# First layer's dispatch loads input rows and normalises them on ACT; first input in four pieces; output weights scaled inside the loop

## The chip, the cores and the metric

The kernel is one program on one core of a Trainium2 chip. The metric is device time in microseconds (us) of the whole program, the median of several runs. All tensors are float32. TensorE is called PE here, VectorE DVE, ScalarE ACT, GpSimd POOL, and SP is the engine that issues most of the DMA transfers.

## What is computed

Two layers, each of the same outer form, on 4096 rows of 256 numbers:

```python
xn = layernorm(x)
x = x + L0_attn(xn, ...) + L0_ffn(xn, ...)     # layer 0
xn = layernorm(x)
x = x + L1_attn(xn, ...) + L1_ffn(xn, ...)     # layer 1
```

`L0_attn` is a state-space mixer: one projection gives a gate (2048 channels), h (2048), B and C (128 each) and a step size dt for each of 32 heads; h, B and C pass a causal convolution of four taps and a silu; dt passes softplus; then a scan over the rows, in which each head's state decays by exp(A dt). The output is multiplied by silu(gate), divided by its root mean square, multiplied by `norm_w` for each channel, and projected by `W_out` to 256.

`L0_ffn` is a mixture of 16 experts. A row goes to the best four experts of its two best groups, and two shared experts take every row:

```python
g = silu(einsum('th,efh->tef', x, w1_e)); u = einsum('th,efh->tef', x, w3_e)
routed = einsum('tef,ehf,te->th', g * u, w2_e, combine)
```

Here x is the normalised row xn. Layer 1 has a linear attention with batch norms and a mixture of 8 experts, two for each row; the change touches it only by a name.

## The kernel before

**The start (0 to about 100 us).** Rows are taken in eight groups of 512, as 128 partitions x 4 tiles x 256. For each group `fetch` (L868) loads the input (`xin`), and `norm_block` (L156) runs in three parts with a `yield` between. First come the mean and variance of each tile on DVE (`st`, `mv`, L162 to L164), a square root on ACT (`rs`, L165), a reciprocal on DVE (L166) and the normalised rows `xn` on DVE (L168). Then `xn` is written to DRAM (`xn_d`, L172) and transposed on PE (`pt`, L176), and ACT copies the result to `xt` (L179), which also goes to DRAM (`xT_d`). Last comes a small projection on PE (`pr`) to 32 step sizes and 16 router scores, which DVE takes out (`take0`). For each quarter of the rows `sizes` (L886) turns the step sizes into decays: `e_t` and `a_row` by exp, `l_t` by ln, `u_t` by exp (L901), then `adt`, `rows` and `dec`. Square root, exp, ln and silu need different tables on ACT. Between these, SP loads the weights (`weights()`), of which `w_o` is the output projection, and `rows_sb`, a small row of constants.

In the start the program's order on SP and DVE is the order of the code (a manual schedule); on ACT, PE and POOL a scheduler sets the order. Before the loop begins, the first projections `pj`, convolutions (`cv` on ACT L371 and DVE L373, then silu to `hc` and `bc`), and `hdt` and `hd` of the first half step are made. At L999 to L1002 POOL multiplies the sixteen slices of `w_o` by `norm_w` (`n_ch`).

**The loop (L1045).** It has 128 half steps: 16 blocks of 256 rows, by four groups of eight heads, by two halves of 128 rows. In each, PE makes projections (`pj` L363, `pg` L433), the state's update (`pst`, in `advance`), the mixer's output (`py` L561) and the output projection (`po` L595); DVE does the taps and a scan (`mm` L468); POOL multiplies `mm` by the B-C products (`masked`, L517), `g` by the gate (`gate_y`, L1019) and `hdt` by its decay (`hd`, L507); SP fetches the decays of later halves (`mm<-step_d`, `cs<-from_d`). Six calls of `point()` in a half step are places where other work is mixed in, and that work has three stages:

- In the first half steps the router's choice runs, with 0 to 2 pieces per point, and large fills of the expert buffers with zeros (one issue per half step).
- From half step 14 (`FILLED`) on, `dispatch0` (L676) advances twice in a half step, at its fourth and sixth point. For each of 32 tiles of 128 rows it loads the normalised rows from `xn_d` into `xs` one tile ahead, POOL copies the row's tail of routing data behind them, and four indirect DMAs, issued by POOL, write the rows to the places of their four experts. One tile takes two half steps.
- When `dispatch0` has ended, the 82 steps of the expert pipeline (79 blocks of 256 rows and 3 to drain it; `blocks`, four generators) are spread over the half steps that are left: `t = ceil(todo / remaining)`, so two per half step at first and one at the end.

```python
elif sends is not None and k >= FILLED:
    points[3], points[5] = sends, sends
elif ticks is not None and todo:
    t = min(todo, -(-todo // max(len(half) - 1 - k, 1)))
```

In the first two stages the code's order holds on POOL and SP, in the third on all engines. An engine takes its instructions in order, so one that waits holds up all behind it. In one half step POOL's order around the change is: `masked` (two `mm`), then `gate_y` of the half step before, then `hd` of the next.

**Behind the loop** the shared experts run (with rows from `xT_d`), then layer 1, whose dispatch loads its rows from `xn_d` at L1255.

Of the kernel before, what the change touches and what calls it, by code (L numbers as in the profile page):

```python
# [10 lines left out]
FP = mybir.dt.float32  # L11
# [90 lines left out]
def two_layer_kernel(  # L102
# [43 lines left out]


    xT_d = [dram.tile([P, KD, FB], FP, name=f"xT_d{g}") for g in range(NFB)]
    xn_d = [[dram.tile([FB, DM], FP, name=f"xn_d{lay}_{g}") for g in range(NFB)] for lay in (0, 1)]

    xg0_d = dram.tile([NB0 * RB, RW0], FP, name="xg0_d")
    xg1_d = dram.tile([NB1 * RB, RW1], FP, name="xg1_d")
# [3 lines left out]
    def norm_block(g, lay, src, work, bank, w_r, n_r, take, xn, xt, copies):  # L156


        mv = work.tile([P, TPB, 2], FP, tag="mv", name=f"mv{g}", bufs=2)
        rs = work.tile([P, TPB], FP, tag="rs", name=f"rs{g}", bufs=2)  # L160
        for j in range(TPB):
            st = work.tile([P, 6], FP, tag="st6", name=f"st{g}_{j}", bufs=4)  # L162
            nc.vector.bn_stats(st, src(j))
            nc.vector.bn_aggr(mv[:, j, :], st)  # L164
        nc.scalar.activation(rs, mv[:, :, 1], AF.Sqrt, bias=eps_t)  # L165
        nc.vector.reciprocal(rs, rs)  # L166
        for j in range(TPB):
            nc.vector.tensor_scalar(  # L168
                xn[:, j, :DM], src(j), mv[:, j, 0:1], rs[:, j : j + 1], ALU.subtract, ALU.mult
            )  # L170
        yield
        nc.sync.dma_start(xn_d[lay][g].rearrange("(j p) d -> p j d", p=P), xn)  # L172
        for k in range(KD):
            pt = bank(f"pt{g}_{k}", False)
            for j in range(TPB):
                nc.tensor.transpose(  # L176
                    pt[:, j * P : (j + 1) * P], xn[:, j, k * P : (k + 1) * P], ident
                )
            copies[k](xt[:, k, :], pt)  # L179
        yield  # L180
        pr = bank(f"pr{g}", True)
        prv = pr.rearrange("p (j n) -> p j n", j=TPB)
        for j in range(TPB):
            for k in range(KD):
                nc.tensor.matmul(
                    prv[:, j, :n_r],
                    xt[:, k, j * P : (j + 1) * P],
                    w_r[:, k, :],
                    start=(k == 0),
                    stop=(k == KD - 1),  # L190
                )
        take(g, prv)
# [109 lines left out]
    from_d = [dram.tile([NTP * HEADS, P], FP, name=f"from_d{p}") for p in range(PARTS)]  # L302
    w_o = wpool.tile([P, NCI, DM], FP, name="w_o")
    sc = wpool.tile([P, NT, E0], FP, name="sc")
    blank = wpool.tile([P, RPB, RW0], FP, name="blank")
    nc.gpsimd.memset(blank, 0.0)
    nc.gpsimd.iota(
# [34 lines left out]
    with tc.tile_pool(name="m", bufs=1) as mp, tc.tile_pool(  # L342
# [169 lines left out]
        def masked(n, j, blk):  # L512

            mm = rows_in[n * CPB + j]
            for q in range(GH // QH):
                m = mm[:, q * QH : (q + 1) * QH, :]
                nc.gpsimd.tensor_tensor(m, m, mid(blk["gm"][j], QH), ALU.mult)  # L517
            return mm
# [157 lines left out]
        def dispatch0():  # L676

            def load(i):
                if i < NT:
                    xs = moe.tile([P, RPB * DM], FP, tag="ys", name=f"xs0_{i}", bufs=3)[:, :RW0]  # L680
                    o = i % TPB * P
                    nc.sync.dma_start(xs[:, :DM], xn_d[0][i // TPB][o : o + P, :])
                    ahead.append(xs)

            ahead = []
            load(0)
            yield
            for i in range(NT):
                load(i + 1)
                xs = ahead.pop(0)  # L690
                nc.gpsimd.tensor_copy(xs[:, DM:], tail0[:, i, :])
                for k in range(TOPK0):
                    nc.gpsimd.indirect_dma_start(
                        out=views0[i * TOPK0 + k],
                        out_offset=bass.IndirectOffsetOnAxis(ap=dest0[:, i, k : k + 1], axis=0),
                        in_=xs,
                        in_offset=None,
                        bounds_check=NB0 * RB - 1,
                    )
                    yield  # L700
# [167 lines left out]
        def fetch(g):  # L868
            if g < NFB:
                t = mp.tile([P, TPB, DM], FP, tag="mm", name=f"xin{g}", bufs=3)  # L870
                nc.sync.dma_start(
                    t, x[g * FB : (g + 1) * FB, :].rearrange("(j p) d -> p j d", p=P)
                )
                xin.append(t)

        def take0(g, prv):
# [119 lines left out]
        ahead()  # L996
        ahead()
        decays(0, 0)
        for c in range(NCI):  # L999
            nc.gpsimd.tensor_scalar(  # L1000
                w_o[:, c, :], w_o[:, c, :], n_ch[:, c : c + 1], 0.0, ALU.mult, ALU.add
            )  # L1002
        for e in early:
            whole(e)
        side.close()
# [10 lines left out]
        def gate_y(k):  # L1016
            if k >= 0:
                n, j = half[k]
                nc.gpsimd.tensor_tensor(  # L1019
                    gs[k], gs[k], gates[n][:, :, j * P : (j + 1) * P], ALU.mult  # L1020
                )
# [23 lines left out]
        for k, (n, j) in enumerate(half):  # L1045
            blk = blks[steps[n][0]]
            next(fill, None)
            points, t = [None] * 6, 0
            if routing is not None:
                for _ in range(3):  # L1050
                    if next(routing, side) is side:
                        side.close()
                        moe = side.enter_context(tc.tile_pool(name="moe", bufs=1))
                        routing, sends = None, dispatch0()
                        break
# [4 lines that stand above are left out]
                if t == 1:  # L1060
                    points[0], points[2], points[4] = ticks[:3]
                else:
                    points = ticks[:3] * t
                todo -= t

            def point():
                nonlocal sends, ticks
                q = points.pop(0)
                if q is not None and next(q, done) is done and q is sends:
                    sends, ticks = None, [blocks(at) for at in range(4)]  # L1070
                    ordered.close()
                    ordered.enter_context(tc.manual_schedule())

            if begun is not None:
                second, begun = begun, None
            else:
                second = None
            conv, gate = (n + 1 + j, 1 - j), (n + j, 1 - j)
            if conv[1] == 0 and conv[0] < len(steps) and steps[conv[0]][1] == 0:
                begun = begin(steps[conv[0]][0])  # L1080
                next(begun)
            late(k - 1)
            ahead()
            old = state[steps[n][1]]
            ahead_of = projections(conv, gate)
            at_once = ticks is not None
            if at_once:
                advance(n, j, blk, made[k][1])
            next(ahead_of, None)
            point()  # L1090
            if not at_once:
                advance(n, j, blk, made[k][1])
            ys[k] = old, masked(n, j, blk)
            gate_y(k - 1)
            if t:
                next(ticks[3])
            if over:
                finish(over.pop())
            next(ahead_of, None)
            point()  # L1100
            next(ahead_of, None)
            if k + 1 < len(half):
                n1, j1 = half[k + 1]
                made[k + 1] = inputs(n1, j1, hcs[n1])
            point()
            next(ahead_of, None)
            if second is not None:
                whole(second)
            next(ahead_of, None)
            if begun is not None:  # L1110
                next(begun)
            point()
            out_ = project(*half[k - 3], gs.pop(k - 3)) if k >= 3 else iter(())
            next(out_, None)
            if begun is not None:
                next(begun)
            point()
            whole(out_)
            if k + 1 < len(half):
                decays(*half[k + 1])  # L1120
            while points:
                point()
            if t > 1:
                next(ticks[3])
# [111 lines left out]
    def route1():  # L1236
# [15 lines left out]
        for g in range(NFB):  # L1252
            tl = slice(g * TPB, (g + 1) * TPB)
            xs = wk.tile([P, TPB, RW1], FP, tag="xs", name=f"xs{g}")
            nc.sync.dma_start(xs[:, :, :DM], xn_d[1][g].rearrange("(j p) d -> p j d", p=P))  # L1255
            nc.gpsimd.memset(xs[:, :, DM:RW], 0.0)
            nc.gpsimd.tensor_copy(xs[:, :, DM], ids_t[:, tl])
            nc.gpsimd.tensor_copy(xs[:, :, RW:], comb1[:, tl, :])
# [341 lines left out]
```

## Time and profile before

| what | value |
|---|---|
| median of three runs | 2353.54 us (2347.74, 2353.54, 2356.76) |
| profiled execution's own time | 2359.07 us |
| its span / granted TensorE clock | 2357.2 us / 0.966 |
| PE busy | 2182.1 us, 93% |
| PE weight load (PEld) busy | 1728.1 us, 73% |
| DVE busy | 1460.2 us, 62% |
| ACT busy | 920.9 us, 39% |
| POOL busy | 1486.4 us, 63% |
| DMA | 412.17 MB, 175 GB/s |

An engine's busy time is the sum of its instructions' durations; its share is an average over stages that differ much. PE's matmul times are modelled, so 93% is not PE at its peak. The span in 40 slices of 59 us shows the stages (each digit is the busy share in tenths):

```profile
PE   6687999999999998999999989999799989999998
DVE  6799988888888887555565656677356542111111
POOL 0345699888888988677777777888541461323222
```

The first two slices are the start and the loop's first half steps. From there to slice 15 or so the rows are routed and sent out; then the expert blocks run beside the mixer until about slice 27; the rest is the shared experts and layer 1. The transfers that the change touches are, in the profile's list of DMA issues (KB each, median us from issue to landing):

```profile
xn_d<-xn SPq DMA_DIRECT2D x16, 512.0 KB, 7.2
xin<-in_x SPq DMA_DIRECT2D x8, 512.0 KB, 5.5
xs<-xn_d SPq DMA_DIRECT2D x32, 128.0 KB, 5.6
```

### The profile page before, as it was taken

How to read it: one execution, taken by the hardware profiler on the slowest of the kernel's cores; microseconds unless marked ns; L12 is line 12 of the kernel's file. 1: busy time of each engine (PE TensorE's matmuls, PEld its weight loads, DVE VectorE, ACT ScalarE, POOL GpSimd, SP SyncE). 2: the span in 40 equal slices, each digit the busy share in tenths (PEclk: the TensorE clock that was granted, in tenths of full speed). 3: DMA queues.
4: the chain of work that ended last, by engine and by line, in shares of the span. 5: the costliest groups of instructions: out<-in, count | busy, mean ns of one | idle time of the engine just before them, and what ended most of it. 6: DMA issues, size and time to landing. Idle time of an engine off the chain costs nothing. (4 is left out here: it accounts for less than half of the span.)

```text
span 2357.2 us, 36770 instructions
## 1 busy us (share of the span) xinstructions
PE 2182.1 (93%) x12684; PEld 1728.1 (73%) x12684; DVE 1460.2 (62%) x3356; ACT 920.9 (39%) x1907; POOL 1486.4 (63%) x1294
## 2 busy tenths in 40 slices
PE   6687999999999998999999989999799989999998
PEld 5565777777777777777777868788566568888887
DVE  6799988888888887555565656677356542111111
ACT  5632443343334333444443434444223752222221
POOL 0345699888888988677777777888541461323222
PEclk8799999999999999999999999999899999999999
DMA  9577679544444445677777777766451347777775
GB/s 307 195 216 213 194 232 259 174 143 153 143 136 155 145 133 169 158 181 165 181 178 168 189 175 176 177 169 164 134 188 54 107 158 215 188 202 189 199 195 116
DMA packets 247435, 412.17 MB, mean 175 GB/s; under 512 B 41552, under 2 KB 184912, under 8 KB 242640
## 3 DMA queue, kind: packets, MB, share of 16 engines
q1 hardware_dynamic: 198240, 347.24, 47.7%
q0 software_dynamic: 42336, 57.04, 13.8%
q10 hardware_dynamic: 6672, 5.51, 0.7%
q8 instruction: 103, 1.69, 0.3%
q14 instruction: 84, 0.69, 0.1%
HBM read 293.19 MB, written 116.52 MB: 174 GB/s over the span
## 5 line engine op out<-in xcount | busy, mean ns | idle before, releaser
L373 DVE SCALAR_TENSOR_TENSOR cv<-pj,cw,cv 128x256 f32<-128x256 f32 x864 | 402.5, 477 | 99.1 <-ACT cv L371 90.0
L517 POOL TENSOR_TENSOR mm<-mm,btok 128x512 f32<-128x512 f32 x256 | 341.6, 1435 | 13.3 <-DVE mm L468 12.5
L468 DVE TENSOR_TENSOR_SCAN mm<-mm,eyes 128x256 f32<-128x256 f32 x512 | 318.0, 667 | 24.3 <-ACT eyes L474 24.3
L363 PE MATMUL pj<-xt,w_in 128*128 128x259 f32 (+1 forms) x1152 | 315.4, 399 | 11.6 <-DVE pj L359 7.3
L433 PE MATMUL pg<-xt,w_in 128*128 128x256 f32 x1024 | 281.7, 397 | 32.3 <-ACT gate L440 29.7
L777 POOL DMA_INDIRECT moe_d<-ys,ids x158 | 248.9, 1575 | 98.4 <-DMA moe_d<-ys,ids 42.3
L1492 POOL DMA_INDIRECT out<-ys,ids x72 | 111.0, 1541 | 301.6 <-ACT ys L1488 267.5
L363 PEld LDWEIGHTS pj<-xt,w_in 128*128 128x128 f32 x1152 | 218.1, 196 | 79.8 <-issue 35.0
L595 PE MATMUL po<-w_o,g 128*128 128x256 f32 x1024 | 261.5, 389 | 0.0
L433 PEld LDWEIGHTS pg<-xt,w_in 128*128 128x128 f32 x1024 | 188.9, 196 | 90.3 <-ACT gate L440 39.2
L1476 DVE TENSOR_TENSOR hid<-silu,pu 128x512 f32<-128x512 f32 x72 | 49.5, 688 | 321.6 <-PE pu L1470 321.6
L371 ACT ACTIVATE cv<-pj,cw 128x256 f32<-128x256 f32 x288 | 135.5, 471 | 240.0 <-PE pj L363 239.4
L507 POOL TENSOR_TENSOR hd<-hdt,dec 128x512 f32<-128x512 f32 x124 | 144.4, 1165 | 121.6 <-DVE hdt L498 117.5
L595 PEld LDWEIGHTS po<-w_o,g 128*128 128x128 f32 x1024 | 193.9, 195 | 28.1 <-issue 2.7
L1019 POOL TENSOR_TENSOR g<-g,gate 128x512 f32<-128x512 f32 x128 | 180.4, 1409 | 50.4 <-DVE g L572 27.6
L384 ACT ACTIVATE hc<-cv,bw 128x256 f32<-128x256 f32 x256 | 129.2, 505 | 160.6 <-DVE cv L373 160.4
L747 PE MATMUL pgu<-xgt,w 128*128 128x256 f32 x632 | 155.6, 390 | 18.6 <-DVE state L543 18.6
L472 DVE TENSOR_TENSOR cs<-cs,eyes 128x512 f32<-128x512 f32 x248 | 159.2, 671 | 0.0
L587 ACT ACTIVATE g<-g 128x512 f32<-128x512 f32 x128 | 80.8, 632 | 200.7 <-POOL g L591 147.6
L572 DVE SCALAR_TENSOR_TENSOR g<-hc,ch,py 128x128 f32<-128x128 f32 x512 | 144.3, 339 | 22.2 <-PE py L561 22.0
L561 PE MATMUL py<-cs,state 128*64 128x128 f32 x1984 | 145.5, 286 | 13.3 <-issue 9.8
L561 PEld LDWEIGHTS py<-cs,state 128*64 128x64 f32 x1984 | 111.3, 141 | 59.8 <-issue 54.3
(245 smaller groups left out, 4063.8 us busy)
## 6 DMA issues: line engine op xcount, KB each, us to landing
mm<-step_d SPq DMA_DIRECT2D x128, 512.0 KB, 5.0
cs<-from_d SPq DMA_DIRECT2D x124, 512.0 KB, 6.1
w<-in_w_ffn SPq DMA_DIRECT2D x36, 1024.0 KB, 5.9
w<-in_w_ffn SPq DMA_DIRECT2D x79, 384.0 KB, 3.3
xg_d<-blank SPq DMA_DIRECT2D x26, 828.0 KB, 9.3
xg<-xg_d SPq DMA_DIRECT2D x79, 260.0 KB, 4.3
w<-in_w_ffn SPq DMA_DIRECT2D x36, 512.0 KB, 6.6
xg_d<-blank SPq DMA_DIRECT2D x18, 536.0 KB, 9.6
```

The costliest lines, as they stand in the source:

```text
L363: nc.tensor.matmul(pj[:, h0 : TB + HALO], w_in[:, k, INTER + c * P : INTER + (c + 1) * P], xts[b][:, k, h0 : TB + HALO], start=(k == 0), s ...
L373: nc.vector.scalar_tensor_tensor(cv, pj[:, i : i + TB], cw[:, c, i : i + 1], cv, ALU.mult, ALU.add)
L433: nc.tensor.matmul(pj[:, :TB], w_in[:, k, c * P : (c + 1) * P], xts[b][:, k, HALO:], start=(k == 0), stop=(k == KD - 1),)
L468: nc.vector.tensor_tensor_scan(m, m, eye, 0.0, ALU.mult, ALU.add)
L472: nc.vector.tensor_tensor(m, m, mid(c_in[:, j, :], QH), ALU.mult)
L507: nc.gpsimd.tensor_tensor(hd, hdt, last(dec[c // NTP][:, 0, c % NTP, hs], HP), ALU.mult)
L517: nc.gpsimd.tensor_tensor(m, m, mid(blk["gm"][j], QH), ALU.mult)
L561: nc.tensor.matmul(py[(h % 2) * HP : (h % 2 + 1) * HP, h // 2, :], left[:, h, :], right[:, h, :], start=(a == 0 and h < 2), stop=(a == len ...
L595: nc.tensor.matmul(po[:, j, :], g[:, i, :], w_o[:, k, :], start=(k == 0 and j == 0), stop=(k == NCI - 1), skip_group_check=True,)
L747: nc.tensor.matmul(pgu[:, a, :], w[:, o : o + P], xgt[:, k, :], start=(k == 0), stop=(k == KD - 1),)
L777: nc.gpsimd.indirect_dma_start(out=moe_d[:, :], out_offset=bass.IndirectOffsetOnAxis(ap=ids[:, j : j + 1], axis=0), in_=ys[:, j, :], in_of ...
L1019: nc.gpsimd.tensor_tensor(gs[k], gs[k], gates[n][:, :, j * P : (j + 1) * P], ALU.mult)
```

## The change

1. `norm_block` writes the normalised rows to DRAM in layer 1 only. In layer 0 two small DVE instructions per group keep `rs` (one over the deviation) and `-mean * rs` of every row in `norm0`.
2. `dispatch0` loads rows of the input x instead of `xn_d`, and ACT normalises them in place (activation Identity with a scale and a bias per row) before they are sent: tile i + 1 after the second send of tile i. The first tile has a step of its own, so the generator has one `yield` more.
3. The first group's input is fetched in four pieces of 128 rows instead of one of 512.
4. The scaling of `w_o` on POOL (16 instructions) moves from ahead of the loop into half step 1, between `masked` and `gate_y`.
5. At L1255 layer 1 reads the renamed `xn_d`.

```diff
@@ norm_block
-        nc.sync.dma_start(xn_d[lay][g].rearrange("(j p) d -> p j d", p=P), xn)
+        if lay:
+            nc.sync.dma_start(xn_d[g].rearrange("(j p) d -> p j d", p=P), xn)
+        else:
+            tl = slice(g * TPB, (g + 1) * TPB)
+            nc.vector.tensor_copy(norm0[:, 0, tl], rs)
+            nc.vector.scalar_tensor_tensor(
+                norm0[:, 1, tl], mv[:, :, 0], -1.0, rs, ALU.mult, ALU.mult
+            )
@@ dispatch0
-                    o = i % TPB * P
-                    nc.sync.dma_start(xs[:, :DM], xn_d[0][i // TPB][o : o + P, :])
+                    nc.sync.dma_start(xs[:, :DM], x[i * P : (i + 1) * P, :])
                     ahead.append(xs)
+
+            def normed(i):
+                if i < NT:
+                    xs = ahead[-1]
+                    nc.scalar.activation(
+                        xs[:, :DM], xs[:, :DM], AF.Identity, bias=norm0[:, 1, i : i + 1],
+                        scale=norm0[:, 0, i : i + 1],
+                    )
 
             ahead = []
             load(0)
+            yield
+            normed(0)
             yield
             for i in range(NT):
                 load(i + 1)
                 xs = ahead.pop(0)
                 nc.gpsimd.tensor_copy(xs[:, DM:], tail0[:, i, :])
                 for k in range(TOPK0):
+                    if k == 2:
+                        normed(i + 1)
                     nc.gpsimd.indirect_dma_start(
@@ fetch
-                nc.sync.dma_start(
-                    t, x[g * FB : (g + 1) * FB, :].rearrange("(j p) d -> p j d", p=P)
-                )
+                v = x[g * FB : (g + 1) * FB, :].rearrange("(j p) d -> p j d", p=P)
+                for j in range(0, TPB, TPB if g else 1):
+                    m = TPB if g else j + 1
+                    nc.sync.dma_start(t[:, j:m, :], v[:, j:m, :])
@@ ahead of the loop
-        for c in range(NCI):
-            nc.gpsimd.tensor_scalar(
-                w_o[:, c, :], w_o[:, c, :], n_ch[:, c : c + 1], 0.0, ALU.mult, ALU.add
-            )
@@ in the loop's half step
             ys[k] = old, masked(n, j, blk)
+            if k == 1:
+
+                for c in range(NCI):
+                    nc.gpsimd.tensor_scalar(
+                        w_o[:, c, :], w_o[:, c, :], n_ch[:, c : c + 1], 0.0, ALU.mult, ALU.add
+                    )
             gate_y(k - 1)
```

More of the change, by code (lines that the diff above doesn't have):

```diff
@@ L148, in two_layer_kernel @@
     xT_d = [dram.tile([P, KD, FB], FP, name=f"xT_d{g}") for g in range(NFB)]
-    xn_d = [[dram.tile([FB, DM], FP, name=f"xn_d{lay}_{g}") for g in range(NFB)] for lay in (0, 1)]
+    xn_d = [dram.tile([FB, DM], FP, name=f"xn_d{g}") for g in range(NFB)]
     xg0_d = dram.tile([NB0 * RB, RW0], FP, name="xg0_d")
@@ L304, in two_layer_kernel @@
     sc = wpool.tile([P, NT, E0], FP, name="sc")
+    norm0 = wpool.tile([P, 2, NT], FP, name="norm0")
     blank = wpool.tile([P, RPB, RW0], FP, name="blank")
@@ L1254, in route1 @@
             xs = wk.tile([P, TPB, RW1], FP, tag="xs", name=f"xs{g}")
-            nc.sync.dma_start(xs[:, :, :DM], xn_d[1][g].rearrange("(j p) d -> p j d", p=P))
+            nc.sync.dma_start(xs[:, :, :DM], xn_d[g].rearrange("(j p) d -> p j d", p=P))
             nc.gpsimd.memset(xs[:, :, DM:RW], 0.0)
```

## The prediction

> **What bounds the kernel now.** I read first the busy time by stretch of the start (columns: stretch, its length, busy us and instructions of five engines, granted clock, share of the DMA engines, GB/s).
>
> ```profile
> 20.00:40.00 20.00, 13.80 (x62) 11.58 (x61) 13.97 (x52) 13.92 (x21) 0.10 (x1) 1.00 1.01 361
> 40.00:60.00 20.00, 13.88 (x69) 11.66 (x68) 11.22 (x42) 12.28 (x20) 0.18 (x2) 0.63 0.94 309
> 80.00:100.00 20.00, 11.38 (x42) 8.32 (x42) 16.86 (x40) 18.47 (x31) 0.10 (x1) 0.83 0.39 118
> 120.00:140.00 20.00, 16.04 (x86) 11.89 (x85) 19.14 (x44) 5.51 (x11) 6.62 (x6) 0.91 0.51 147
> ```
>
> Until 80 us the transfers are full and no engine is, so the start looks bound by transfers. The waits of 0 to 105 us (us in total, times, longest) deny it:
>
> ```profile
> PE pt L176 <- DVE xn L168: 13.5, 4, 9.4
> DVE e_t L903 <- ACT u_t L901: 9.7, 4, 4.7
> DVE rs L166 <- ACT rs L165: 9.4, 8, 2.4
> DVE st L163 <- DMA xin<-in_x: 4.7, 1, 4.7
> ACT xt L179 <- DMA xT_d<-xt: 1.3, 2, 0.8
> ```
>
> TensorE waits for VectorE, VectorE for ScalarE, ScalarE for its tables. A transfer holds an engine of this chain only at the very start (4.7) and for 1.3 us in all. The start is a chain of small steps, and the order on ACT decides. Third, ACT's instructions in order of time (start, us):
>
> ```profile
> 22.36 0.30 ACT L165 ACTIVATE rs<-mv,eps_t 128x4 f32<-128x4 f32 x1 [4.13 <-DVE mv L164]
> 22.91 1.07 ACT L179 COPY xt<-pt 128x512 f32<-128x512 f32 x2 [0.25 <-PE pt L176]
> 24.00 1.28 ACT L894 ACT_TABLE_LOAD   x1
> 25.30 0.42 ACT L894 ACTIVATE e_t<-e_t 128x256 f32<-128x256 f32 x1
> 25.73 1.28 ACT L165 ACT_TABLE_LOAD   x1
> 27.12 0.30 ACT L165 ACTIVATE rs<-mv,eps_t 128x4 f32<-128x4 f32 x1
> 27.96 1.07 ACT L179 COPY xt<-pt 128x512 f32<-128x512 f32 x2 [0.55 <-DMA xT_d<-xt]
> ```
>
> rs of block 3 goes ahead of the copies of xt 2, and rs of block 4 (27.12) ahead of both copies of xt 3. Fourth, POOL at the loop's first halves, and the later stages by hundred us:
>
> ```profile
> 111.23 2.48 POOL L517 TENSOR_TENSOR mm<-mm,btok 128x512 f32<-128x512 f32 x2
> 114.19 1.59 POOL L1019 TENSOR_TENSOR g<-g,gate 128x512 f32<-128x512 f32 x1 [0.48 <-DVE g L572]
> 116.54 1.42 POOL L507 TENSOR_TENSOR hd<-hdt,dec 128x512 f32<-128x512 f32 x1 [0.76 <-DVE hdt L498]
> 130.14 1.27 POOL L1019 TENSOR_TENSOR g<-g,gate 128x512 f32<-128x512 f32 x1 [9.30 <-DVE pj L359]
> ```
>
> ```profile
> 600.00:700.00 100.00, 95.40 (x641) 75.16 (x642) 84.31 (x186) 37.10 (x82) 87.05 (x83) 0.95 0.42 139
> 1300.00:1400.00 100.00, 94.50 (x580) 76.33 (x579) 59.63 (x127) 43.31 (x110) 78.14 (x60) 0.98 0.74 182
> 1500.00:1600.00 100.00, 98.24 (x658) 81.64 (x659) 75.45 (x160) 46.09 (x108) 83.75 (x67) 1.00 0.67 165
> ```
>
> TensorE, VectorE and POOL are all near full while rows are sent out (600); with expert blocks, two per half step (1300) wait more than one per half step (1500).
>
> **The change part by part.** Instruction orders are those of the built programs, durations those of the profiled run.
>
> *No normalised rows written.* Eight transfers of 512 KB go, 4.19 MB, at the 306 GB/s mean of 0 to 80 us 13.7 us of transfer. But engines waited 1.3 us for transfers, of which 0.55 lies ahead of l_t on the chain; in the new order both copies come behind other waits. Value 0, between -1.3 and 0. The rival below says what if transfers decide.
>
> *16 small VectorE operations for norm0.* Nearest rows: 128x3 copies 0.15, reciprocal 0.18; at most 16 x 0.18 = 2.9. They stand before VectorE's waits for TensorE or ACT (2.48 at 30.0, 2.58 at 40.2, 3.65 at 58.6), which cover them. Value 0, up to 2.
>
> *First input in four pieces.* Four issues instead of one put rows_sb's issue at 0.83 + 4 x 0.47 + 0.50 = 3.2 instead of 1.87. ACT's first instruction waits for rows_sb (until 5.82) and the first rs is queued behind it, so VectorE's earlier statistics (to 1.6 earlier) gain little. The same bytes lie ahead of rows_sb: I let it land at 6.1; then eyes, table 6.7 to 8.0, rs 8.0 instead of 8.31: -0.3. A rule speaks against it: the Trainium skill, "DMA: Bandwidth & Descriptors", section "Bandwidth", asks for batches of 1 MiB and lists 64 KB at 138 GB/s; estimated from that, four pieces one after another take 3.8 us where the row's 512 KB landed 3.8 after issue[...], and rs would be about 1.3 later. The row is nearer (issue 0.47, landing 3.8). Range -1.4 to +1.3.
>
> *A new order on ACT in the start.* The schedule now has rs 3 behind the copies of xt 2, and the first copy of xt 3 ahead of e_t, whose table load and rs 4 stand behind it. On PE, pr 2 now runs whole ahead of pt 3; before, they were mixed, 23.55 to 28.59, so pt 3 ends there. Then: copy 28.4 to 29.0, table to 30.3, e_t to 30.7, second copy to 31.3, table to 32.6, rs 4 at 32.6 instead of 27.12: +5.5. After it xn 4 ends at 34.5 and u_t at 37.5 instead of 32.50, since one of two tables is now loaded while ACT would wait: +5.0. From there the order is as before up to block 7, so it stays. Bounds +3 to +6.
>
> *Two more table loads.* 88 instead of 86. At 67 us cv 16 moves ahead of u_t: it waits for pj until 67.64, so u_t ends at 69.8 instead of 67.13 and adt at 72.7 instead of 69.23; then bc 16 and 17 are split around rows, with 1.28 twice more: dec ends at 76.0 instead of 72.72, e_t of part 3 at 79.1 instead of 76.25: +2.8, carried on by an ACT 18.47 of 20 us busy. The Trainium skill, "ScalarE: Activation LUTs", section "What ACT_TABLE_LOAD costs", gives 1283 ns plus a drain of 1380, 2.66 a switch; here the next activation starts 1.30 after the load's start (24.00, 25.30). By the row two loads are 2.6, by the page 5.3; I take the row. Range 1 to 4.
>
> *Scaling of w_o in the loop.* Before: 16 x 0.48 = 7.7 us on POOL, 71.1 to 78.8, under a POOL that was idle to 94: free. Now behind mm of half step 1, which ended at 113.7: g of half step 0 moves from 114.19 to 121.5, hd from 116.54 to 122.9. PE, in order, needs that g for a po and then hd for pst; it got to pst at 121.19 and gets there at 124.1: +2.9, passed to VectorE (19.14 of 20 busy). POOL's idle 9.30 ahead of 130.14 covers the rest. Value +3; 0 if VectorE has slack, 7.7 with no cover.
>
> *Normalising on ACT.* 32 activations of 128x256, like gate or hc, 0.47 to 0.50: 16 us on an engine 37 to 40% busy, no table load in the order. The row is loaded a half step (10.2 us) ahead, landing took 5.6, so nothing waits for it; POOL's sends come another half step later. What stands behind it on ACT (cv, hc, gate) comes 0.5 later. From 500 to 900 us VectorE waited 26.4 and 20.8 us for ACT and PE 13.2: 60 of 400. 15% of 16 is +2.4; 0 to 16.
>
> *One step more in the dispatch.* One more yield: the expert blocks start at half step 80 instead of 79, so one half step has neither sends nor blocks, and 35 instead of 34 have two blocks, 12 instead of 14 have one. By POOL's gates: 10.20 us with sends, 17.02 with two blocks, 11.53 with one. 10.20 + 17.02 - 2 x 11.53 = +4.2; without sends the half step is shorter, at least 8.5 (one block's half less its 3 us of matmuls): +2.5. Value +3.5.
>
> Sum: -0.3 + 5.0 + 2.8 + 3.0 + 2.4 + 3.5 = +16.4. The profiled run took 2359.07 (span 2357.2 and 1.9 around it) and would take 2375.5; it lies 5.5 above the median, so 2353.5 + 16.4 = 2370.
>
> **Rivals.** *Transfers decide the start* (faster, 15%): at 0 to 65 us, 13.7 us less traffic comes through whole, the order on ACT being paid out of waits that vanish. It decides if block 7's xn or the first pj comes earlier than 58 and 65 us. For: 1.01 and 0.94 DMA share. Against: 1.3 us of waits. With the later +3.5 left: 2343, or 2335 if w_o and Identity cost nothing and four pieces give 1.4. *The start's delay is swallowed* by VectorE's and ACT's slack before 100 us (25%): only w_o, ACT and the steps remain, +9: 2362. *ACT's 32 activations are all on the path* (10%): +13.6 more, 2384. *The four pieces do nothing*, because rows_sb holds the first rs: in the sum nearly so already. My forecast: 50%.
>
> **How the numbers follow.** A measurement here tells 0.5%, 11.8 us, from none: 2342 to 2365. Forecast and its terms' bounds give 2357 to 2383, mostly slower; the swallowed start is mostly same; the transfer rival is mostly faster. Faster 0.12, same 0.30, slower 0.58. The range takes in the upper transfer case and most of the ACT case: 2343 to 2384.
>
> **What would show it.** rs of block 4 near 32.6 and xn 7 later than 58; e_t of part 3 about 8 later; the first POOL hd of the loop near 108 instead of 100.08; 16 w_o operations between mm and g with PE's pst 3 late; half steps of 10.2 to 10.3 in the dispatch; 35 of 17.0. Wrong if the loop begins before 100 us, or if a dispatch half step changes by over 0.1 us, since 64 of them make 6.

## The result and the profile after

The changed kernel takes 2381.77 us (median of four, 2375.55 to 2391.62) where the kernel before takes 2352.25 (four, 2347.74 to 2356.76): a ratio of 1.0124, 95% interval 1.0097 to 1.0152, or 29.5 us more. The forecast was 16.4 more. Its profiled execution took 2375.55 (span 2373.8), within 0.1 us of the 2375.5 that the prediction worked out for it. That is chance: this execution is the lowest of the four after, as the one before lay above its median, and the sum was made of terms of which several were too small.

Busy time by stretch of the changed kernel, to be held against the same stretches of before:

```profile
20.00:40.00 20.00, 11.57 (x51) 10.14 (x51) 11.34 (x47) 10.07 (x15) 0.00 (x0) 1.00 0.62 217
40.00:60.00 20.00, 13.02 (x59) 10.79 (x59) 12.13 (x47) 11.72 (x18) 0.29 (x2) 0.70 0.92 303
80.00:100.00 20.00, 12.64 (x44) 10.64 (x44) 4.49 (x15) 13.42 (x19) 0.10 (x1) 0.55 0.29 91
120.00:140.00 20.00, 13.31 (x69) 8.98 (x68) 18.73 (x43) 2.33 (x5) 15.73 (x20) 0.67 0.50 146
```

From 20 to 40 us the transfers fell from 1.01 to 0.62 of their engines, and every compute engine became emptier with them. The start was not bound by transfers. From 80 to 100 VectorE does 4.49 us of work where it did 16.86: all is later. From 120 to 140 POOL is busy 15.73 instead of 6.62, which is the scaling of w_o.

The waits of 0 to 105 us:

```profile
PE pt L183 <- DVE xn L168: 20.4, 5, 10.4
DVE rs L166 <- ACT rs L165: 18.4, 8, 4.5
DVE e_t L923 <- ACT u_t L921: 12.6, 4, 7.6
DVE st L163 <- DMA xin<-in_x: 2.9, 1, 2.9
```

The wait for the first input is shorter (2.9 after 4.7), as the first of four pieces lands earlier. The chain of small steps waits longer: VectorE 18.4 for roots on ACT instead of 9.4, TensorE 20.4 for xn instead of 13.5. ACT in order of time shows why:

```profile
23.90 1.07 ACT L186 COPY xt<-pt 128x512 f32<-128x512 f32 x2 [4.68 <-PE pt L183]
24.86 0.31 ACT L165 ACTIVATE rs<-mv,eps_t 128x4 f32<-128x4 f32 x1
29.85 0.59 ACT L186 COPY xt<-pt 128x512 f32<-128x512 f32 x1 [4.68 <-PE pt L183]
30.45 1.28 ACT L914 ACT_TABLE_LOAD   x1
31.75 0.42 ACT L914 ACTIVATE e_t<-e_t 128x256 f32<-128x256 f32 x1
32.07 0.57 ACT L186 COPY xt<-pt 128x512 f32<-128x512 f32 x1
32.66 1.28 ACT L165 ACT_TABLE_LOAD   x1
33.95 0.30 ACT L165 ACTIVATE rs<-mv,eps_t 128x4 f32<-128x4 f32 x1
```

The copies of xt 2 now stand ahead of rs 3 (24.86 instead of 22.36), and a copy of xt 3 that waits 4.68 us for TensorE stands ahead of e_t and, behind it, rs 4 (33.95 instead of 27.12). POOL at the loop's first halves:

```profile
117.54 1.04 POOL L515 TENSOR_TENSOR hd<-hdt,dec 128x512 f32<-128x512 f32 x1 [5.71 <-DVE hdt L506]
...
128.68 2.48 POOL L525 TENSOR_TENSOR mm<-mm,btok 128x512 f32<-128x512 f32 x2
131.15 10.80 POOL L1113 TENSOR_SCALAR w_o<-w_o,ch 128x256 f32<-128x256 f32 x16
141.91 1.26 POOL L1035 TENSOR_TENSOR g<-g,gate 128x512 f32<-128x512 f32 x1
143.13 1.04 POOL L515 TENSOR_TENSOR hd<-hdt,dec 128x512 f32<-128x512 f32 x1
144.13 2.48 POOL L525 TENSOR_TENSOR mm<-mm,btok 128x512 f32<-128x512 f32 x2
154.05 1.27 POOL L1035 TENSOR_TENSOR g<-g,gate 128x512 f32<-128x512 f32 x1 [7.44 <-DVE pj L367]
```

In the kernel before, the first hd and the work on w_o were here:

```profile
71.09 7.70 POOL L1000 TENSOR_SCALAR w_o<-w_o,ch 128x256 f32<-128x256 f32 x16
100.08 1.04 POOL L507 TENSOR_TENSOR hd<-hdt,dec 128x512 f32<-128x512 f32 x1 [5.71 <-DVE hdt L498]
```

The loop's first hd is 17.46 us late. The w_o work takes 10.80, and the second gate (g<-g,gate) is at 154.05 instead of 130.14, 23.9 late, so w_o added 6.45. From there the 128 gate instructions of POOL, one per half step and here counted from 0, are a clock for the whole loop. How late each is against the same gate of before, in us, from the two traces:

| gate | 2 | 12 | 40 | 76 | 78 | 82 | 112 | 115 | 127 |
|---|---|---|---|---|---|---|---|---|---|
| late by | 23.9 | 23.9 | 21.4 | 16.4 | 20.7 | 6.2 | 4.2 | 17.0 | 17.0 |

Nothing is lost or won until the dispatch begins (behind gate 12). The fall of 10 from 76 to 82 is the half step that has no blocks, and the rise at 112 to 115 the doubled half step that comes for it.

### The profile page after: what moved, and what is told of

It is laid out like the page before. It is cut to its first block, busy times and chain, and to the rows that moved or that the text cites. A ratio compares the mean times of both kernels' runs of the same rounds, so it can differ in the third digit from the quotient of the medians.

```text
span 2373.8 us, 36906 instructions
## 1 busy us (share of the span) xinstructions
PE 2189.9 (92%) x12684; PEld 1729.4 (73%) x12684; DVE 1458.8 (61%) x3372; ACT 938.0 (40%) x1941; POOL 1486.8 (63%) x1294
## 5 line engine op out<-in xcount | busy, mean ns | idle before, releaser
L525 POOL TENSOR_TENSOR mm<-mm,btok 128x512 f32<-128x512 f32 x256 | 341.6, 1436 | 12.1 <-DVE mm L476 11.3
L371 PE MATMUL pj<-xt,w_in 128*128 128x259 f32 (+1 forms) x1152 | 322.3, 406 | 12.7 <-DVE pj L367 8.7
L766 PEld LDWEIGHTS pgu<-xgt,w 128*128 128x128 f32 x632 | 122.6, 198 | 46.1 <-DVE state L551 28.3
L448 ACT ACTIVATE gate<-pg,b_ch 128x256 f32<-128x256 f32 x256 | 120.0, 469 | 83.9 <-PE pg L441 79.1
```

The source lines that it names most:

```text
L371: nc.tensor.matmul(pj[:, h0 : TB + HALO], w_in[:, k, INTER + c * P : INTER + (c + 1) * P], xts[b][:, k, h0 : TB + HALO], start=(k == 0), s ...
L766: nc.tensor.matmul(pgu[:, a, :], w[:, o : o + P], xgt[:, k, :], start=(k == 0), stop=(k == KD - 1),)
```

## The experiments

Theory A: the start's delay is the order of instructions on ACT, w_o's delay is the queue behind it on POOL, and both are carried to the end. Theory B: the loop's slack swallows such delays, and the time comes from the dispatch (the activations on ACT, or the step more). Within the start, the rivals to the order were the late landing of rows_sb, the norm0 instructions' own time, and TensorE's clock.

The experiments were run in three groups; the runs of one group shared a chip. On these chips the kernel before took 2391.5 to 2398.2 us, and in every profile taken there the stage behind the loop (last gate to end of span) is 35 to 43 us longer than in the first profile. So times are given as ratios to before of the same group, and positions inside the loop as trace times. The first group:

**w_o alone.** Before, with the change's own lines:

```diff
-        for c in range(NCI):
-            nc.gpsimd.tensor_scalar(w_o[:, c, :], ...
...
             ys[k] = old, masked(n, j, blk)
+            if k == 1:
+                for c in range(NCI):
+                    nc.gpsimd.tensor_scalar(w_o[:, c, :], ...
```

> The kernel before, with only the scaling of w_o moved into half step 1. Theory (three separate costs that add up): the start is untouched, the first POOL hd stays within 0.3 us of 100.08, the sixteen instructions take about 10.8 us beside a busy VectorE and delay the gate of half step 2 by 6.4 us (from 130.14 to about 136.5), and the whole takes about 6 us more (2358). Rival (POOL and VectorE have slack in the routing steps that takes it back): the gate of half step 2 is late, but by half step 14 less than 2 us is left, and the time is that of before within 3 us. My prediction's own term was +3.

Ratio 1.0036 (1.0017 to 1.0054), 8.6 us. The scaling on POOL and the gates around it:

```profile
116.05 10.79 POOL L1093 TENSOR_SCALAR w_o<-w_o,ch 128x256 f32<-128x256 f32 x16
126.82 1.26 POOL L1015 TENSOR_TENSOR g<-g,gate 128x512 f32<-128x512 f32 x1
128.04 1.04 POOL L507 TENSOR_TENSOR hd<-hdt,dec 128x512 f32<-128x512 f32 x1
129.03 2.48 POOL L517 TENSOR_TENSOR mm<-mm,btok 128x512 f32<-128x512 f32 x2
139.59 1.27 POOL L1015 TENSOR_TENSOR g<-g,gate 128x512 f32<-128x512 f32 x1 [8.08 <-DVE pj L359]
```

The first hd was at 102.45, not within 0.3 of 100.08: the start itself varies by some 2 us between runs. From hd to gate 2 it took 7.07 more than before. The gates stay 9.3 to 9.4 late to gate 43, so the loop's slack swallowed nothing there: A. By gate 127 they are 5.8 late.

**Pieces alone.** Before, with fetch(0) in four:

```diff
+                for j in range(0, TPB, TPB if g else 1):
+                    m = TPB if g else j + 1
+                    nc.sync.dma_start(t[:, j:m, :], v[:, j:m, :])
```

> The kernel before, with only the first input fetched in four pieces. Theory: rows_sb lands 1.0 to 1.7 us later and holds ACT's first instructions; the first rs starts at 9.3 instead of 8.31 and everything in the start is later by that 1.0, the first hd at 101.1; the time is +1, which the rounds cannot tell from none. Rival (the statistics are ready earlier, so the start gains): rs no later than 8.3, hd at or before 100.1.

Ratio 1.0013 (0.9997 to 1.0029). rs started at 9.02, near the 9.3 of the theory, and hd at 102.50, 1.4 later than it said. But w_o alone, without pieces, had 9.14 and 102.45. So this pair shows no cost; the landing of rows_sb varies. What holds the first root's table load is seen in ACT's instructions, in the kernel before and with the pieces:

```profile
5.82 0.23 ACT L896 ACTIVATE a_row<-rows_sb 128x32 f32<-128x32 f32 x1 [3.71 <-DMA rows_sb<-in_rows]
7.01 1.28 ACT L165 ACT_TABLE_LOAD   x1 [0.69 <-DVE mv L164]
```

```profile
7.20 0.23 ACT L897 ACTIVATE a_row<-rows_sb 128x32 f32<-128x32 f32 x1 [5.09 <-DMA rows_sb<-in_rows]
7.72 1.28 ACT L165 ACT_TABLE_LOAD   x1
```

In the kernel before it is VectorE's statistics (mv), by 0.69 us; with the pieces it is a_row, and so rows_sb. All runs in which a_row stands first: without pieces rs starts at 8.31, 9.14, 8.39, 8.64 and 8.38 (mean 8.57), with pieces at 9.30, 9.02, 9.09, 9.50, 10.18 and 10.75 (mean 9.64). By these means the pieces cost about 1.1 us, though the two groups overlap.

**Dispatch part alone.** After, with the fetch and w_o as before:

```diff
-                for j in range(0, TPB, TPB if g else 1):
...
-            if k == 1:
...
         decays(0, 0)
+        for c in range(NCI):
```

> The kernel before, with only the dispatch part (no xn_d write in layer 0, norm0, rows of x normalised on ACT, one step more). Theory: this part alone brings the new order on ACT in the start; the first hd at about 116.5 (16.5 of the 17.46 us), the gate of half step 12 at +16.5 and the time about 17 to 20 us more (2370). Rival (the order comes from the pieces or from POOL's missing w_o work, and the dispatch part costs only ACT's 32 activations and the step): hd below 103, the time +3 to +6 (2357).

Ratio 1.0086 (1.0068 to 1.0104), 20.6 us; first hd at 113.43, 11 later than in the two runs above. ACT has the order of the changed kernel up to the loop. A, though by less than expected (116.5); the rest goes with TensorE's clock, below.

**The old order in the changed kernel.** `behind` adds a dependency without a semaphore, which only fixes who stands first in ACT's queue. The three places are the root, the copies of xt and the silu to bc:

```diff
+            if g == 4:
+                behind(r, ("e_t", 0))
...
+            if not lay and g in (2, 3):
+                behind(r, ("rs", g + 1))
+            if not lay and g == 4:
+                behind(r, ("u_t", 0))
...
+            if b == 0 and c >= NCI:
+                behind(r, ("dec", 2))
```

> The changed kernel, whole, with the old order on ACT in the start held by dependencies that cost no wait on the engine (rs 3 and 4 ahead of the copies of xt 2 and 3, u_t ahead of xt 4, both bc behind dec). Theory (the order is the cost): the first hd goes from 117.54 back to 101 to 105 and the time falls by 13 to 16 us, to about 2366. Rival (the sixteen norm0 instructions, the later landings or PE's lower granted clock are the cost, and the order only follows): hd stays above 110 and the time falls by less than 7.

First hd at 107.39, between the two bands; rs 4 at 28.19 and u_t at 32.49 are back at the times of before (27.12, 32.08). It is 4.9 later than in the run with the pieces alone (102.50). Of this 2.7 is the one instruction that I left in its new place, cv 16 ahead of u_t of part 2: against before, u_t there is 6.15 late where the copy ahead is 3.43 late. No run isolates the rest. The ratio is 1.0088 (1.0069 to 1.0107), 21.1 us, only 3 to 8 us less than the changed kernel's 24 to 29, where 13 to 16 were expected. The order is confirmed in the start, but the time fell by less than the start did. By the traces, its last gate comes 6.2 us earlier than in the second profile of the changed kernel (below), of 7.2 us won in the start. Against the first profile of after it comes 2.8 later, though 10.2 were won: the loop's later stages spread as much as that between executions (table below).

The second group, all with the changed kernel beside them:

**The changed kernel again**, unedited.

> The changed kernel once more, beside the runs of this call. Theory: 1.2% over before (+29 us), the first hd 13 to 15.5 us later than in the two kernels whose start was not touched (102.45), and a gap at half step 79 followed by a doubled step more at 113 to 114. Rival (the first profile's PE clock of 0.53 was part of the change): the first hd again 17 us late or more with the same low clock.

Ratio 1.0102 (1.0071 to 1.0133), 24.4 us; hd at 114.56, 2.98 earlier than in the first profile and 12.1 later than 102.45, a little under the 13 to 15.5 expected.

**One step less**, in the changed kernel:

```diff
             yield
             normed(0)
-            yield
```

> The changed kernel with the dispatch's extra step taken out again (the first tile is normalised in the step in which its first sends go). Theory (the step costs what the gates show): expert blocks start at half step 79 as before, 34 doubled steps instead of 35; the sum of the fall at 76 to 82 and the rise at 112 to 115, which was +2.6, goes to 0, and the time falls by 2 to 3 us, near what the rounds can tell. Rival (the shift of the blocks by a half step slows all doubled steps, which drifted by -2 to +10 us in the profiles): the time falls by 6 to 10 us.

Ratio 1.011 (1.0082 to 1.0138), against 1.0102: no gain by time. In the trace the blocks start a half step earlier and the rise at 112 is gone; from gate 76 to 127 this execution was 8.0 us shorter than before, the changed kernel beside it 6.7 longer. But the profiles are of two executions at the ends of the spread: their own times are 2412.93, the second lowest of its six, and 2425.87, the second highest of its six, 12.9 apart. So this difference shows how executions spread and not what the edit does. By time, with six runs each and an error of some 8 us, neither the theory's 2 to 3 nor 0 is excluded; the rival's 6 to 10 lies at the edge or beyond.

**No activation**, in the changed kernel:

```diff
             def normed(i):
-                if i < NT:
+                if i < 0:
```

> The changed kernel without the 32 activations: rows of x are sent out as they are, not normalised, so the experts work on other numbers. Theory (ACT has room in the dispatch): half steps 16 to 76 take what they take with the activations within 1 us in sum, and the time is within 3 us of the changed kernel's. Rival (part of the 16 us is on the path, which I had priced at 2.4): 2 to 16 us less, seen as shorter dispatch half steps.

Ratio 1.0095 (1.0063 to 1.0127); median 2416.87 against 2416.37 with the activations. They cost nothing that shows, but the error of this difference is some 9 us: the rival's 16 is out, the predicted 2.4 is not. Nor do the traces tell whether they cost less than 1 us. In the dispatch (gate 2 to 76) the six executions with them take 3.2 us less than before on average (from 7.6 less to 0.8 more), the six others with the old dispatch 1.8 less, this one 6.0 less.

**w_o one half step later**, on before:

```diff
-            if k == 1:
+            if k == 2:
```

> The kernel before with the scaling of w_o in half step 2 instead of half step 1, behind masked, where POOL sat idle for 8.4 to 9.3 us ahead of the gate. Theory (the cost is the wait of g, hd and PE behind it on POOL; where POOL idles it is hidden): the gate of half step 2 is 1 to 3 us late instead of 6.5 to 7, and the time +2. Rival (VectorE[...] is slowed by the sixteen instructions wherever they run): 5 us or more as in half step 1.

Ratio 1.0018 (0.9999 to 1.0036). The scaling now runs where POOL sat idle:

```profile
118.33 3.32 POOL L517 TENSOR_TENSOR mm<-mm,btok 128x512 f32<-128x512 f32 x2
121.63 11.27 POOL L1093 TENSOR_SCALAR w_o<-w_o,ch 128x256 f32<-128x256 f32 x16
132.86 1.27 POOL L1015 TENSOR_TENSOR g<-g,gate 128x512 f32<-128x512 f32 x1
```

It takes no less (11.27), and gate 2 is 2.16 late against hd, instead of 7.07. The price was the place in the queue. The time alone (4.3 us, from 0 to 8.6) would not decide between theory and rival.

The last group:

**norm0 alone**: before, plus two instructions per group behind the write of xn.

```diff
+        if not lay:
...
+            nc.vector.tensor_copy(norm0[:, 0, tl], rs)
+            nc.vector.scalar_tensor_tensor(norm0[:, 1, tl], ...
```

> The kernel before with only the sixteen small VectorE instructions for norm0 added (nothing reads norm0; the rows are still written, and the dispatch is the old one). Theory (the scheduler orders ACT by its own estimate of when inputs are ready, and these sixteen are enough to turn it): the built program has the new order in most places, and the first hd comes at 110 to 113 instead of 100.1 to 102.5, though the sixteen take 2.7 us in all. Rival (the missing xn_d transfers and their places on SP bring the delay): hd at most 3 us later than in the kernel before.

Ratio 1.0066 (1.0042 to 1.009), 15.8 us; first hd at 115.65, and all 128 gates 14 to 19 us late. The loop's first hd, in the old-order run and in this one:

```profile
107.39 1.04 POOL L535 TENSOR_TENSOR hd<-hdt,dec 128x512 f32<-128x512 f32 x1 [5.71 <-DVE hdt L526]
```

```profile
115.65 1.04 POOL L514 TENSOR_TENSOR hd<-hdt,dec 128x512 f32<-128x512 f32 x1 [5.71 <-DVE hdt L505]
```

Sixteen instructions of 0.15 to 0.16 us, whose results nobody reads, bring the whole delay of the start. In the built program ACT's order is that of the changed kernel but for one copy of xt 2 ahead of rs 3 instead of two, and e_t ahead of both copies of xt 3, with rs 4 between them. That the scheduler's estimates of readiness turned it is argued; that these instructions are enough is shown.

**a_row later**: before, with a_row behind rs 3 by the same kind of dependency; nothing else changes place on ACT or PE.

```diff
-                nc.scalar.activation(a_row, rows_sb[:, 2 * HEADS :], AF.Exp)
+                behind(nc.scalar.activation(a_row, rows_sb[:, 2 * HEADS :], AF.Exp), ("rs", 3))
```

> The kernel before with a_row held behind the fourth root on ACT (everything else on ACT and PE stands in the order of before). Theory (the first root waits for rows_sb through a_row, which stands ahead of it): the square root's table is loaded while nothing waits, the first rs starts at about 7.0, when its statistics are there, instead of 8.3 to 9.1, and the first hd is 1.5 us earlier than 100.1 to 102.5. Rival (the statistics or the transfer of xin are the bound): rs at 8.3 or later.

**The same, with the four pieces.**

> As the run with a_row held back, and the first input in four pieces. Theory: now the pieces are worth something, as the statistics are ready at 5.4 and nothing else holds the root: first rs at about 5.5, the first hd at 97 to 99.5, the time 3 us below that of before (0.1%, which the rounds can hardly tell). Rival (the pieces do nothing here either): rs as in the run without them, near 7.0.

For the run without pieces the expectation failed. ACT's first instructions there:

```profile
2.12 0.38 ACT L351 COPY eyes<-ident 128x256 f32<-128x256 f32 x1
7.16 1.28 ACT L167 ACT_TABLE_LOAD   x1 [4.66 <-DVE mv L166]
8.45 0.30 ACT L167 ACTIVATE rs<-mv,eps_t 128x4 f32<-128x4 f32 x1
```

The table load stands behind a wait for VectorE's statistics, which end at 7.07; ACT idles 4.66 us in front of it. rs is no earlier than 8.31, and the first hd, at 103.20, no earlier either (ratio 1.0012, 0.9995 to 1.0029). The same with the pieces:

```profile
5.48 1.28 ACT L167 ACT_TABLE_LOAD   x1 [2.98 <-DVE mv L166]
6.78 0.30 ACT L167 ACTIVATE rs<-mv,eps_t 128x4 f32<-128x4 f32 x1
```

Now the earlier statistics count: rs at 6.78, the first hd at 98.79, the earliest of all 14 profiles. The ratio is 0.9993 (0.9977 to 1.0009): not told from none.

**The change mended**: the changed kernel with the edits of four runs above (old order held, a_row behind rs 3, w_o at k == 2, one `yield` less).

> The changed kernel with its costs taken away: the old order on ACT held (except for the first cv, 2.7 us), a_row behind the fourth root, w_o scaled in half step 2, one dispatch step less. Theory (order, w_o and rows_sb are the whole cost): first rs at 5.5, first hd at 100 to 104, the gate of half step 2 another 2.3 later, and the time within 5 us of the kernel before instead of 24 to 29 above it. Rival (something in the dispatch that no run isolated costs 8 us or more): the time stays 0.4% or more above before.

rs at 6.74, first hd at 103.74 (cv 16 is again in its new place), 2.10 more to gate 2. Ratio 1.0036 (1.0019 to 1.0052), 8.6 us: two thirds of the change's cost are gone, but the theory's 5 us lies near the lower end of the interval (4.5 to 12.4), and the rival's 0.4% is not excluded. None of the runs shows a version that beats the kernel before beyond the error.

## Why the prediction was right or wrong, step by step

The direction, the range (to 2384) and the bound were right: a chain of small steps with ACT's order deciding. The 16.4 was too small because three terms were: the second of the two for the order on ACT (both together 7.8, where 12.5 to 15.5 was measured), w_o (3.0, where 7.2 was) and the pieces (-0.3, where +1.1 was). That the range held the result is in part luck. The upper bounds of all terms but the activations' (norm0 2, pieces 1.3, order 6, loads 4, w_o 7.7, step 4.2) sum to 25.2, less than the 29.5 of the first measurement (the second, 24.4, lies just under it). The room above came from the 16 allowed to the activations, whose cost does not show; with it the bounds reach 2395, not the 2383 stated.

All profiles, in us. The three columns with signs are differences from the first profile of before; gates are counted from 0:

| kernel | first rs | first hd | hd to gate 2 | gate 2 to 76 | gate 76 to 127 | ratio |
|---|---|---|---|---|---|---|
| before | 8.31 | 100.08 | 0 | 0 | 0 | 1 |
| after | 9.30 | 117.54 | +6.4 | -7.6 | +0.6 | 1.0124 |
| w_o alone | 9.14 | 102.45 | +7.1 | -1.8 | -1.8 | 1.0036 |
| pieces alone | 9.02 | 102.50 | -0.9 | -1.7 | +1.3 | 1.0013 |
| dispatch alone | 8.39 | 113.43 | -0.6 | -4.4 | +12.4 | 1.0086 |
| old order | 9.09 | 107.39 | +8.1 | -2.4 | +6.8 | 1.0088 |
| after again | 9.50 | 114.56 | +7.8 | -2.9 | +6.7 | 1.0102 |
| one step less | 10.18 | 115.50 | +7.3 | +0.8 | -8.0 | 1.0110 |
| no activation | 10.75 | 119.90 | +6.6 | -6.0 | +6.1 | 1.0095 |
| w_o later | 8.64 | 100.47 | +2.2 | -2.1 | +0.1 | 1.0018 |
| norm0 alone | 8.38 | 115.65 | -0.5 | -0.4 | +0.4 | 1.0066 |
| a_row later | 8.45 | 103.20 | -0.9 | -0.4 | -8.4 | 1.0012 |
| a_row later, pieces | 6.78 | 98.79 | -1.5 | -4.6 | -4.9 | 0.9993 |
| mended | 6.74 | 103.74 | +2.1 | -2.9 | +4.2 | 1.0036 |

**No rows written: 0.** Right. The transfers fell by 4.19 MB and nothing came earlier, so the transfer rival is out.

**norm0: 0, covered by VectorE's waits.** As put, this failed. Their own time is covered (with the old order held, the second rows of part 1 are at 56.16, against 56.57 with the pieces alone), but they alone turn ACT's order. I had read the new order from the built program and priced it apart, so it was in the sum, under another name.

**Four pieces: -0.3.** Measured +1.1. The step that failed is "I let it land at 6.1": rows_sb let a_row start at 7.2 to 8.9 with pieces, at 5.8 to 7.3 without. Nor did rows_sb hold the first rs in the profile before, as I had read it: the statistics did, by 0.69, so with rows_sb on time the pieces would have gained. The estimate from the rule on batching (1.3) came near in size, but not by its path: it had the pieces themselves finish later, while their last statistics ended at 5.38 (after) where the whole block's ended at 6.93.

**New order, first half: +5.0.** Right: dispatch alone against pieces alone, u_t of part 0 is 37.58 against 32.93, +4.65, and rs 4 +5.2 where I had 5.5.

**Two more loads: +2.8.** Mis-sized; by the same pair the lead grows from 4.65 to 10.9. Of it 1.7 comes before any of the steps I listed (the last root and the copies behind it), 2.7 from u_t behind cv 16, as I had it, 0.95 to the rows behind the split bc, and 1.0 more to e_t of part 3. On top of that comes TensorE's clock. The sixteen matmuls of pr 7 lie on this chain, in the dispatch run and in the norm0 run:

```profile
86.44 1.88 PE L192 MATMUL pr<-w_small,xt 128*128 128x48 f32 x16
```

```profile
85.22 3.49 PE L191 MATMUL pr<-w_small,xt 128*128 128x48 f32 x16
```

Where they take 1.88 or 2.50 (three profiles) it is 105.0 to 105.3 us from the first rs to the first hd; where they take 3.49 (after, no activation, norm0) it is 107.3 to 109.2. With the old order it is 91.8 to 93.5, and pr 7 took 1.99 in each of these four (with a_row moved as well, 94.8 and 92.0). So the order costs 12.5 us, and some 3 more in the executions in which the clock is low at that moment; that the clock is their cause is argued. I took the clock as given. The Trainium skill, "TensorE: Matmul & The Clock Gate", section "What's actually happening", says that the window of the clock gate runs freely and does not start anew with a kernel, so that the moment of the switch varies from run to run. The traces agree: while pr 7 ran, the granted clock was 0.50 in the first profile of after, 0.74 in the second profile of the same kernel, and 1.00 in the dispatch run.

**w_o: +3, at most 7.7.** Measured 7.2 (mean of six). Two things failed: the duration, 10.8 to 11.2 instead of 7.7, and the cover. I let 9.30 us of idle POOL ahead of the gate cover what was left, but 7.44 of it stays in the profile after. The gate there waits for VectorE, and so, I argue, for the chain over g, hd and TensorE's queue that w_o itself delayed.

**Activations: +2.4.** Measured 0, with an error of some 9. They took 0.60 each, more than the 0.50 I gave them, and none of it shows; 2.4 lies within the error. My sign of being wrong, a dispatch half step changed by over 0.1 us, did come up in the first profile, but as a gain: -7.6 from gate 2 to 76, which is -0.12 for each of the 64 half steps of the dispatch. In the six executions with activations it is -0.05 on average, with the old dispatch -0.03, so no cost shows there; why the executions differ is not found.

**One step more: +3.5.** Open in size. The fall at 76 to 82 and the rise at 112 to 115 sum to 2.5 on average in the five executions that have the step, to 0.5 in the nine that do not: 2.0 for what I had priced at 3.5. But the whole stage from 76 to 127 is +6.5 with it (0.6 to 12.4) and -1.9 without (-8.4 to +4.2). That would be 8.4, with an error of some 2.3 from the spread, and the run with one step less gained nothing by time (1.0110 against 1.0102, an error of some 8 us). Another way to it: dispatch alone (20.6 us) less norm0 alone (15.8) leaves 4.8, with an error of some 7, for the step, the activations and the missing writes together, where I had 5.9. What slows doubled half steps from execution to execution is not found.

Sum of the measured: order and clock 12.5 to 15.5, pieces 1.1, w_o 7.2, step 2 to 8: 23 to 32, where the two measurements say 29.5 and 24.4. The swallowed-start rival is out: norm0 alone keeps its 15 us to the last gate. The rival in which all activations are on the path is out too, though its time, 2384, lay close. One sum was wrong without bearing on this: the transfer rival's 13.7 less and 3.5 more give 2343 with w_o and the activations already at nothing, so with the pieces' 1.4 its lower case is 2342, not 2335.

## What to carry to other kernels

Where a scheduler orders an engine, the smallest edit beside it can reorder the queue: read the new order and walk it to the end of the stage, with TensorE's clock at its low and its high value, and expect a delay of an in-order chain to reach the end unless a run shows slack. Work moved into a loop costs what is queued behind it, not its duration; idle time of that engine covers it only if the idle does not itself wait for what is being delayed. And an input that lands earlier is worth nothing while another instruction stands ahead of its consumer.

## What the hardware showed unexpectedly

- A table load on ACT can be held by a wait of its activation. With a_row out of the way ACT was idle from 2.50, yet the load of the root's table started at 7.16, behind the statistics. The trace has a wait for VectorE as an instruction of its own at 7.11, ahead of the load, while the root waits for a second semaphore. The kernel before has the same at 6.96, ahead of the load at 7.01. For block 6 of the kernel before the root has one wait only; there the load ran at once and the root alone waited:

```profile
44.21 1.28 ACT L165 ACT_TABLE_LOAD   x1
45.73 0.30 ACT L165 ACTIVATE rs<-mv,eps_t 128x4 f32<-128x4 f32 x1 [0.24 <-DVE mv L164]
```

- The same 16 instructions took 7.70 us on POOL ahead of the loop, while VectorE was busy for 3.91 of them, and 10.8 to 11.7 in the loop. In the profile of after nine of them take 0.47, and seven 0.84 to 1.26. Each of the seven overlaps a tensor-tensor operation of the router on VectorE with both inputs in SBUF (`ms`, `cmpe`, `ranke`); beside tensor-tensor operations that read one input from PSUM (`state<-state,pst`, `hdt<-pth,dt_sb`) they stay at 0.47. The Trainium skill, "SBUF — State Buffer", section "Who interferes with whom", says that a VectorE instruction with two SBUF inputs contends with a GpSimd instruction that reads SBUF, and the trace agrees. In four other runs one instruction takes 2.53.
